# W in two transfers, gathered rows turned by every fourth column, and one store for row blocks 28 and 29

## The chip, the cores and the metric

The kernel runs on one core of a Trainium2 chip. The metric is the device time of one execution in microseconds (us). Before the change it is 235.61 us, the median of three runs (235.59 to 236.09).

## The reference

The reference is one layer of graph attention with four heads, a residual and a layer norm. `x` is 4096x512, `adj` 4096x4096, `W` 512x2048 (four heads of 512 columns) and `a` holds two vectors of 512 for each head, all fp32.

```python
ht = (h @ W).reshape(N, N_HEADS, N_HIDDEN).transpose(1, 0, 2)
src = jnp.einsum('hnd,hd->hn', ht, a_src)
dst = jnp.einsum('hnd,hd->hn', ht, a_dst)
e = jax.nn.leaky_relu(src[:, :, None] + dst[:, None, :], SLOPE) + adj_mat[None]
att = jax.nn.softmax(e, axis=-1)
h_prime = jnp.einsum('hij,hjd->hid', att, ht)
return h_prime.mean(axis=0)
...
x = _layernorm(x + _L0_gnn_ref(x, adj, L0_gnn_W, L0_gnn_a), axis=-1)
```

The entries of `adj` reach 1e9, so in nearly every row the softmax gives all its weight to the column with the largest entry. For such a row i with column j the result is `layernorm(x[i] + x[j] @ mean_of_heads(W))`.

## The kernel before, in words

`leading_rows` uses this. It finds the largest entry of each row of `adj`, gathers the row of `x` that it points to, multiplies it with the mean of W over the heads, adds `x` and normalises. At the end it tests whether the lead of the largest entry is large enough to make the softmax exact. Only if a row fails is `general` entered (L546 and following), which computes the attention in full; in these runs it is not.

**Row blocks.** The 4096 rows are 32 row blocks of 128. Row block `ib` holds in partition p the row 32p + ib. One loop over `t` from 0 to 31 is a pipeline written out by hand, without a scheduler: at step `t`

- SP (SyncE's queue) issues the load of `adj` block t + 5 (`load_adj`, L122: 2 MB, 16 KB in each partition) and, at some steps, a load of several row blocks of `x` (`load_x`, L125) into the long-lived tile `hold`. There are six buffers for `adj`; a load waits until VectorE is done with the block that was in its buffer.
- VectorE takes maxima of segments of 16 or 32 columns (`segment_maxima`, L169), finds the best segment (`find_segment`, L176 and L178), and from the segment fetched for block t - 2 the column (`find_column`, L208 and L214).
- GpSimd (POOL) fetches the best segment again (`fetch_segment`, L191) and gathers the rows of `x` into `y` (`gather_rows`, L202), both with an indirect DMA on its own queue. There are four buffers for `y`.
- TensorE turns block t - 3 (`turn`, L229: four transposes of 128x128), ScalarE copies the result to `yt` (L231), and TensorE adds the residual (`residual`, L237) and multiplies with `w_sum` (`products`, L244).
- ScalarE takes the sums for the layer norm and normalises (L266, L268, L251, L277), with GpSimd's help (L271 to L273).

**W.** W is loaded at the start into the upper half of `hold`, row blocks 16 to 31, which `x` overwrites later. It comes in four transfers of 1 MB (`load_w`, L128): transfer kb brings rows 128kb + p of W, one row of 8 KB in each partition p. `mean_of_heads(kb)` (L334, L335) adds its four heads on TensorE and writes `w_sum[:, kb]`. `turn_w` (L350) and `head_vector` (L358) form W times `a`, one (kb, head) at a time; `head_norms` (L364 and following) uses only their norms over all rows of W. `products` multiplies `yt[:, kb]`, the columns 128kb to 128kb + 127 of the gathered rows, turned, with `w_sum[:, kb]`, the rows of W of the same numbers.

**Order on SP at the start.** `adj` 0, W 0, `adj` 1, W 1, `adj` 2, W 2, `adj` 3, W 3, `adj` 4, `x` 0 to 3, then the loop's. ScalarE's queue carries two small loads of `a`. The transfers of both queues take eight completion semaphores in turn, so each waits until the one eight before it has landed.

**The tail.** After the loop the last blocks are written out by hand. Row block 31's column is found directly in the whole row (L222), its rows are gathered, turned and multiplied in two halves (`products_of_half`, L286), and normalised in halves by VectorE and ScalarE (L326). SP issues the stores (L329) in one fixed order: row blocks 0 to 7 in two stores of four, 8 to 23 in eight of two, then 28 alone, 29 alone, 24 and 25, 26 and 27, 30, and last 31. A row block of a store is 2 KB in each partition. The names at the tail are NB = 32, Q = 4, LATE = NB - Q = 28 and BEHIND = LATE - Q = 24.

Of the kernel before, what the change touches and what calls it, by code (L numbers as in the profile page):

```python
# [20 lines left out]
P = 128  # L21
# [7 lines left out]
def gat_resnorm_kernel(  # L29
# [29 lines left out]
    any_bad = keep.tile([1, 1], I32, name="any_bad")  # L59

    leading_rows(tc, x, adj, W, a, out, ident, v, n_bad, any_bad)

    flag = nc.values_load(any_bad[0:1, 0:1], min_val=0, max_val=N)
    with tc.If(flag > 0, preferred_fallthrough_block=True, label="general"):
        general(tc, x, adj, W, out, ident, v, n_bad)
# [3 lines left out]
def leading_rows(ctx, tc, x, adj, W, a, out, ident, v, n_bad, any_bad):  # L69
# [8 lines left out]
    nc = tc.nc  # L78
    N, D = x.shape
    H = a.shape[0]  # L80
    KB, NB, S = D // P, N // P, N // E
    S_EARLY = N // E_EARLY
    AHEAD = 5
    Q = 4
    PIECES = 4
    LATE = NB - Q
    BEHIND = LATE - Q
# [11 lines left out]
    adj_segs_early = adj.rearrange("n (s e) -> (n s) e", e=E_EARLY)  # L99
    x_rows = x.rearrange("(p nb) d -> p nb d", nb=NB)  # L100
    out_rows = out.rearrange("(p nb) d -> p nb d", nb=NB)
    w_blocks = W.rearrange("(kb p) (h d) -> p kb h d", p=P, h=H)


    once.tile([P, 24], F32, name="pad")
    hold = once.tile([P, NB, D], F32, name="hold")
    w_at = NB - KB * H
# [6 lines left out]
    def pieces(ib):  # L114
        return PIECES if ib == NB - 1 else 2 if ib >= LATE else 1

    def load_adj(ib):
        if 0 <= ib < NB:
            t = adj_t[ib] = adj_pool.tile([P, N], F32, name="adj_t")
            n = pieces(ib)  # L120
            for k in range(n):
                nc.sync.dma_start(t[:, ts(k, N // n)], adj_rows[ib][:, ts(k, N // n)])  # L122

    def load_x(lo, n):
        nc.sync.dma_start(hold[:, ds(lo, n), :], x_rows[:, ds(lo, n), :])  # L125

    def load_w(kb):
        nc.sync.dma_start(hold[:, ds(w_at + kb * H, H), :], w_blocks[:, kb])  # L128

    load_adj(0)  # L130
    for s in range(2):
        nc.scalar.dma_start(a_rows[ts(s, H), :], a[:, ts(s, D), :].rearrange("h d o -> h (d o)"))
    for kb in range(KB):
        load_w(kb)
        load_adj(kb + 1)
    load_x(0, Q)
    for ib in range(KB + 1, AHEAD):
        load_adj(ib)

    make_identity(nc, ident)  # L140
    first = once.tile([P, NB], U32, name="first")
# [83 lines left out]
    def turn(ib):  # L225
        y = y_t.pop(ib)
        tp = psum.tile([P, KB, P], F32, name="tp", bufs=2)
        for kb in range(KB):
            nc.tensor.transpose(tp[:, kb, :], y[:, ts(kb, P)], ident)  # L229
        yt = yt_of[ib] = rows.tile([P, KB, P], F32, name="yt")  # L230
        nc.scalar.copy(yt, tp)  # L231

# [89 lines left out]
    def finish_in_halves(ib):  # L322

        halves, i = o_ps.pop(ib), slice(ib, ib + 1)
        normalise(ib, halves[0], slice(0, D // 2))
        nc.scalar.activation(hold[:, ib, D // 2 :], halves[1], AF.Identity, bias=nm[:, i], scale=sd[:, i])  # L326

    def store(queue, lo, n):
        queue.dma_start(out_rows[:, ds(lo, n), :], hold[:, ds(lo, n), :])  # L329
# [93 lines left out]
    for t in range(NB):  # L423
# [29 lines left out]
        ib = t - PROJECT  # L453
# [6 lines left out]
        if ib >= 0:  # L460
            turn(ib)
            if ib > BEHIND:
                products(ib - 1, KB - 1, KB)
            if ib < BEHIND:
                residual(ib)
# [25 lines left out]
    add_x(nc.gpsimd, BEHIND + 2)  # L491
    products(LATE, KB - 1, KB)
    turn(NB - 3)
    residual_in_halves(NB - 1)
    products(NB - 3, 0, 1)
# [11 lines left out]
    bound(3)  # L507
    test()
    turn(NB - 2)
    stats(BEHIND + 2)  # L510
    rstd(slice(BEHIND, BEHIND + 3))
# [25 lines left out]
    moments(NB - 1)  # L537
    factor(NB - 1, shift=True)
    finish_in_halves(NB - 1)
    for ib, n in ((NB - 4, 1), (NB - 3, 1), (BEHIND, 2), (BEHIND + 2, 2), (NB - 2, 1)):  # L540
        store(nc.sync, ib, n)
    store(nc.sync, NB - 1, 1)

# [2 lines left out]
def general(ctx, tc, x, adj, W, out, ident, v, n_bad):  # L546
# [7 lines left out]
    nc = tc.nc  # L554
    N, D = x.shape
    KB, NB, NCH, Q = D // P, N // P, N // C, C // P
    H = v.shape[2] // 2

    const = ctx.enter_context(tc.tile_pool(name="const", bufs=1))
    x_sb = const.tile([P, NB, D], F32, name="x_sb")  # L560
# [4 lines left out]
    w_blocks = W.rearrange("(kb p) m -> p kb m", p=P)  # L565

    with ExitStack() as pre:
        sd_all = pre.enter_context(tc.tile_pool(name="all", bufs=1)).tile([2 * H, N], F32, name="sd_all")
        two = pre.enter_context(tc.tile_pool(name="two", bufs=2))
        pps = pre.enter_context(tc.tile_pool(name="pps", bufs=2, space=bass.MemoryType.PSUM))  # L570
        for g in range(NCH):
            nc.gpsimd.dma_start(x_sb[:, ts(g, Q), :], x_blocks[:, ts(g, Q), :])
        for kb in range(KB):
            nc.gpsimd.dma_start(w_sb[:, kb, :], w_blocks[:, kb, :])
        for g in range(NCH):
            xT = two.tile([P, KB, C], F32, name="xT")
            for q in range(Q):
                ps = pps.tile([P, KB, P], F32, name="ps_x")
                for kb in range(KB):
                    nc.tensor.transpose(ps[:, kb, :], x_sb[:, g * Q + q, ts(kb, P)], ident)  # L580
                nc.scalar.copy(xT[:, :, ts(q, P)], ps)
            ps = pps.tile([2 * H, C], F32, name="ps_sd")
            for kb in range(KB):
                nc.tensor.matmul(ps, v[:, kb, :], xT[:, kb, :], start=(kb == 0), stop=(kb == KB - 1))
            sd = sd_all[:, ts(g, C)]
            nc.vector.tensor_copy(sd, ps)
            for h in range(H):
                pb = pps.tile([P, C], F32, name="ps_b")
                one_hot = ident[: 2 * H, H + h : H + h + 1].to_broadcast([2 * H, P])
                nc.tensor.matmul(pb, one_hot, sd, start=True, stop=True)  # L590
                nc.vector.tensor_copy(dst_b[:, h, ts(g, C)], pb)
        for g in range(NCH):
            pt = pps.tile([P, Q, 2 * H], F32, name="ps_s")
            for q in range(Q):
                rows_of = sd_all[:, ds(g * Q + q, P, NB)]
                nc.tensor.transpose(pt[:, q, :], rows_of, ident[: 2 * H, : 2 * H])
            nc.vector.tensor_copy(src[:, ts(g, Q), :], pt[:, :, :H])
# [98 lines left out]
```

## Time and profile before

| | before |
|---|---|
| median of the runs | 235.61 us (235.59 to 236.09) |
| the profiled execution, whole | 235.65 us |
| its span, first to last instruction | 234.1 us |
| TensorE (PE) busy | 197.5 us, 84% |
| VectorE (DVE) busy | 191.6 us, 82% |
| ScalarE (ACT) busy | 111.6 us, 48% |
| GpSimd (POOL) busy | 100.3 us, 43% |
| DMA, mean rate over the span | 415 GB/s |
| median time from issue to landing, W | 18.8 us |
| median time from issue to landing, `adj`, 2 MB | 31.7 us |
| median time from issue to landing, gather of `y` | 7.7 us |

How to read the profile: it is one execution, and times in it count from its span's start. A page gives the busy time of each engine, then the span in 40 equal slices in which a digit is the busy share in tenths, then the DMA queues (packets, megabytes, share of the time of the 16 transfer engines). A group of instructions has its line, engine, operation, output and inputs, sizes and count; behind the first bar the busy time in us and the mean in ns; behind the second the engine's idle time just before, with what ended it. PEld is TensorE's loading of the stationary operand, which overlaps its matmuls. A row of the timeline has its start, its length, engine, line, operation and tiles, and in brackets the idle time before it and what ended that. The chain of waits is followed back from the last instruction, each step to what released it; its rows have start, length and what was waited for or worked on.

### The profile page before, as it was taken

The numbers are of one execution on the slowest core, as the hardware profiler recorded it, in microseconds if no ns is written. First come the engines' busy times: TensorE is split into PE (matmuls) and PEld (weight loads), VectorE is DVE, ScalarE is ACT, GpSimd is POOL, SyncE is SP. The second block draws the span as 40 slices with busy tenths as digits, with TensorE's granted clock in tenths as the row PEclk, the third lists the DMA queues.
The fourth block names the chain that finished last, engine by engine and source line by source line (L and its number), as shares of the span: only waits on it lengthen the run. The fifth ranks groups of instructions, "written<-read, shape, count | busy, mean of one in ns | idle before, by whom it ended". The sixth has DMA issues, their size and how long they took to land.

```text
span 234.1 us, 2486 instructions
## 1 busy us (share of the span) xinstructions
PE 197.5 (84%) x683; PEld 101.6 (43%) x683; DVE 191.6 (82%) x300; ACT 111.6 (48%) x267; POOL 100.3 (43%) x212
## 2 busy tenths in 40 slices
PE   0198959999999699999999599859899967999980
PEld 0034525765656356555544144324333423344360
DVE  0566885589929999999789986999999999989871
ACT  2003012155665447475768264645564654187561
POOL 2022232415524464646443642646465464557400
PEclk9999778999999999999999979999999999999997
DMA  6999999999999999999999999999999999999994
GB/s 243 432 428 417 445 419 434 418 444 420 433 422 427 430 424 433 426 419 431 434 427 427 429 433 424 419 436 419 435 428 417 425 427 421 413 426 419 416 386 179
DMA packets 12977, 97.06 MB, mean 415 GB/s; under 512 B 2072, under 2 KB 2584, under 8 KB 7200
## 3 DMA queue, kind: packets, MB, share of 16 engines
q1 hardware_dynamic: 9360, 88.08, 89.0%
q0 software_dynamic: 3584, 8.77, 9.5%
q8 instruction: 6, 0.10, 0.2%
q14 instruction: 11, 0.09, 0.1%
q10 hardware_dynamic: 16, 0.02, 0.0%
HBM read 88.47 MB, written 8.39 MB: 414 GB/s over the span
## 4 chain that ended last, share of the span: by engine, by line
DMA 48%; POOL 19%; issue 17%; DVE 11%; PE 2%; ACT 0%; POOLq 0%; DVEq 0%; ACTq 0%; SPq 0%
DMA adj_t<-in_adj_dram 41%; DVE seg L169 8%; POOL y L202 6%; POOL lead L191 5%; DMA y<-in_x_dram,col 3%; DMA lead<-in_adj_dram,row 2%; POOL sd L272 2%; PE o L286 2%; DMA a_rows<-in_L_gnn_a_dram 1%; DVE col L222 1%; POOL row L185 1%; POOL start L198 1%; POOL col L216 1%; POOL lead_early L191 1%; DVE at L178 1%
## 5 line engine op out<-in xcount | busy, mean ns | idle before, releaser
L169 DVE TENSOR_REDUCE seg<-adj_t 128x128 f32<-128x2048 f32 (+2 forms) x66 | 145.4, 2207 | 29.0 <-DMA adj_t<-in_adj_dram 29.0
L244 PE MATMUL o<-w_sum,yt 128*128 128x512 f32 x248 | 116.0, 609 | 0.7 <-ACT yt L231 0.7
L244 PEld LDWEIGHTS o<-w_sum,yt 128*128 128x128 f32 x248 | 44.8, 193 | 53.9 <-issue 42.4
L231 ACT COPY yt<-tp 128x512 f32<-128x512 f32 x32 | 18.8, 587 | 45.8 <-PE tp L229 45.7
L202 POOL DMA_INDIRECT y<-in_x_dram,col x32 | 30.8, 961 | 16.5 <-POOL col L216 15.4
L334 PE MATMUL o<-hold,ident 128*128 128x512 f32 x32 | 20.9, 815 | 14.6 <-DMA hold<-in_L_gnn_W_dram 14.6
L229 PE MATMUL tp<-ident,y 128*128 128x128 f32 x128 | 19.7, 276 | 13.7 <-DMA y<-in_x_dram,col 13.7
L237 PE MATMUL o<-hold,ident 128*128 128x512 f32 x52 | 26.8, 600 | 0.0
L229 PEld LDWEIGHTS tp<-ident,y 128*128 128x128 f32 x128 | 14.4, 141 | 26.8 <-issue 25.5
L185 POOL TENSOR_TENSOR row<-at,first 128x1 uint32<-128x1 uint32 x32 | 6.0, 188 | 43.7 <-DVE at L178 43.3
L352 ACT COPY wt<-tp 128x512 f32<-128x512 f32 x16 | 9.2, 586 | 31.5 <-PE tp L350 31.5
L191 POOL DMA_INDIRECT lead_early<-in_adj_dram,row x18 | 18.1, 1008 | 8.9 <-POOL row L185 8.9
L216 POOL TENSOR_TENSOR col<-start,within 128x1 uint32<-128x1 uint32 x31 | 5.8, 188 | 36.0 <-DVE within L214 36.0
L251 ACT ACTIVATE sq<-hold 128x512 f32<-128x512 f32 x32 | 19.8, 619 | 0.0
L358 PEld LDWEIGHTS pv<-at_d,wt 128*128 128x128 f32 x128 | 16.3, 191 | 6.8 <-ACT wt L352 3.7
L334 PEld LDWEIGHTS o<-hold,ident 128*128 128x128 f32 x32 | 8.1, 265 | 25.1 <-issue 20.2
L335 ACT ACTIVATE w_sum<-o 128x512 f32<-128x512 f32 x4 | 2.4, 598 | 33.0 <-PE o L334 33.0
L277 ACT ACTIVATE hold<-o,nm,sd 128x512 f32<-128x512 f32 x24 | 17.2, 769 | 0.0
L191 POOL DMA_INDIRECT lead<-in_adj_dram,row x14 | 14.0, 1003 | 7.0 <-POOL row L185 7.0
L268 ACT ACTIVATE sq<-o,nm 128x512 f32<-128x512 f32 x24 | 16.5, 687 | 0.8
L358 PE MATMUL pv<-at_d,wt 128*128 128x2 f32 x128 | 15.3, 244 | 0.6 <-ACT wt L352 0.6
L266 ACT ACTIVATE sq<-o 128x512 f32<-128x512 f32 x24 | 14.6, 609 | 0.0
(91 smaller groups left out, 150.8 us busy)
## 6 DMA issues: line engine op xcount, KB each, us to landing
adj_t<-in_adj_dram SPq DMA_DIRECT2D x28, 2048.0 KB, 31.7
adj_t<-in_adj_dram SPq DMA_DIRECT2D x6, 1024.0 KB, 28.0
out_dram<-hold SPq DMA_DIRECT2D x10, 512.0 KB, 14.3
hold<-in_L_gnn_W_dram SPq DMA_DIRECT2D x4, 1024.0 KB, 18.8
hold<-in_x_dram SPq DMA_DIRECT2D x2, 2048.0 KB, 36.5
hold<-in_x_dram SPq DMA_DIRECT2D x3, 1024.0 KB, 27.8
adj_t<-in_adj_dram SPq DMA_DIRECT2D x4, 512.0 KB, 19.7
out_dram<-hold SPq DMA_DIRECT2D x2, 1024.0 KB, 13.8
```

What stands on the lines that cost most here:

```text
L169: nc.vector.tensor_reduce(seg_of[ib][:, ts(k, N // e // n)], adj_t[ib][:, ts(k, N // n)].rearrange("p (s e) -> p s e", e=e), axis=AX.X, op ...
L191: nc.gpsimd.indirect_dma_start(out=lead, out_offset=None, in_=adj_segs_early if early else adj_segs, in_offset=bass.IndirectOffsetOnAxis(a ...
L202: nc.gpsimd.indirect_dma_start(out=y, out_offset=None, in_=x, in_offset=bass.IndirectOffsetOnAxis(ap=col[:, :1], axis=0),)
L229: nc.tensor.transpose(tp[:, kb, :], y[:, ts(kb, P)], ident)
L231: nc.scalar.copy(yt, tp)
L237: nc.tensor.matmul(o_ps[ib], ident, hold[:, ib, :], start=start, stop=False)
L244: nc.tensor.matmul(o_ps[ib], yt_of[ib][:, kb, :], w_sum[:, kb, :], start=(start and kb == 0), stop=(kb == KB - 1),)
L251: nc.scalar.activation(sq, hold[:, ib, :], AF.Square, accum_out=xx[:, ib : ib + 1])
L268: nc.scalar.activation(sq, o, AF.Square, bias=nm[:, i], accum_out=sd[:, i])
L277: nc.scalar.activation(hold[:, ib, :], o_ps.pop(ib), AF.Identity, bias=nm[:, i], scale=sd[:, i])
L334: nc.tensor.matmul(o, ident, hold[:, w_at + kb * H + h, :], start=(h == 0), stop=(h == H - 1))
L358: nc.tensor.matmul(pv[:, kb, h : 2 * H : H], wt[:, k, :], at_d[:, k, h : 2 * H : H], start=(k == 0), stop=(k == KB - 1),)
```

## The change

W's row 4p + kb now lies in partition p as its block kb, so that each partition's four rows are 32 KB in one piece. Two transfers of 2 MB bring two blocks each, 16 KB in each partition; `adj` 1 stands between them, and `adj` 2, 3, 4 and the first load of `x` behind them. To match, `turn` takes for its transpose kb the columns kb, kb + 4, kb + 8 and so on of the gathered rows, instead of 128 neighbouring ones (and `general` does the same with `x`). The stores of row blocks 28 and 29 become one.

```diff
-    w_blocks = W.rearrange("(kb p) (h d) -> p kb h d", p=P, h=H)
+    w_blocks = W.rearrange("(p kb) (h d) -> p (kb h) d", p=P, h=H)
...
-    def load_w(kb):
-        nc.sync.dma_start(hold[:, ds(w_at + kb * H, H), :], w_blocks[:, kb])
+    def load_w(kb, n):
+        nc.sync.dma_start(hold[:, ds(w_at + kb * H, n * H), :], w_blocks[:, ds(kb * H, n * H), :])
...
-    for kb in range(KB):
-        load_w(kb)
-        load_adj(kb + 1)
+    for kb in range(0, KB, 2):
+        load_w(kb, 2)
+        load_adj(kb // 2 + 1)
+    for ib in range(KB // 2 + 1, AHEAD):
+        load_adj(ib)
     load_x(0, Q)
-    for ib in range(KB + 1, AHEAD):
-        load_adj(ib)
...
-            nc.tensor.transpose(tp[:, kb, :], y[:, ts(kb, P)], ident)
+            nc.tensor.transpose(tp[:, kb, :], y[:, ds(kb, P, KB)], ident)
...
-    for ib, n in ((NB - 4, 1), (NB - 3, 1), (BEHIND, 2), (BEHIND + 2, 2), (NB - 2, 1)):
+    for ib, n in ((LATE, 2), (BEHIND, 2), (BEHIND + 2, 2), (NB - 2, 1)):
         store(nc.sync, ib, n)
...
-                    nc.tensor.transpose(ps[:, kb, :], x_sb[:, g * Q + q, ts(kb, P)], ident)
+                    nc.tensor.transpose(ps[:, kb, :], x_sb[:, g * Q + q, ds(kb, P, KB)], ident)
```

## The prediction

> **What bounds the kernel now.** I read the page's slices first, then its groups, then the chain of waits, then the timeline around the edited lines.
>
> ```profile
> DMA  6999999999999999999999999999999999999994
> DMA packets 12977, 97.06 MB, mean 415 GB/s; under 512 B 2072, under 2 KB 2584, under 8 KB 7200
> q1 hardware_dynamic: 9360, 88.08, 89.0%
> q0 software_dynamic: 3584, 8.77, 9.5%
> ...
> L169 DVE TENSOR_REDUCE seg<-adj_t 128x128 f32<-128x2048 f32 (+2 forms) x66 | 145.4, 2207 | 29.0 <-DMA adj_t<-in_adj_dram 29.0
> L229 PE MATMUL tp<-ident,y 128*128 128x128 f32 x128 | 19.7, 276 | 13.7 <-DMA y<-in_x_dram,col 13.7
> L229 PEld LDWEIGHTS tp<-ident,y 128*128 128x128 f32 x128 | 14.4, 141 | 26.8 <-issue 25.5
> ```
>
> The transfer engines are full from the second slice to the last but one: 89.0% plus 9.5% of the span is packet time. SP's queue (q1) is served in order, so a block of `adj` lands when all bytes ahead of it have passed. VectorE waits for nothing else in L169 (29.0 us in 13 waits), and TensorE waits for gathered rows. So the kernel is bound by the byte stream, with VectorE (191.6 us busy) close behind, and after the stream by a serial tail. The chain's end shows that tail:
>
> ```profile
> 204.23 5.55 DMA lead<-in_adj_dram,row
> ...
> 215.40 7.09 DMA y<-in_x_dram,col
> 222.49 0.14 issue
> 222.62 0.63 PE tp L229 x4
> 223.25 0.86 PE o L244 x2
> 224.11 3.55 PE o L286 x16
> ```
>
> Nothing else hides the four transposes of row block 31 (0.63 us); the last store is issued at 229.70, when its data is ready.
>
> Where does the stream hand over to the tail?
>
> ```profile
> 182.02 2.29 DVE L169 TENSOR_REDUCE seg<-adj_t 128x64 f32<-128x2048 f32 x1 [0.31 <-DMA adj_t<-in_adj_dram]
> ```
>
> This is block 27: VectorE waited 0.31 us for it, and from here runs without a wait until block 30's segment is found at 203.4, which releases the fetch at 204.23. So an earlier landing of block 27 moves the end one for one, up to 0.31 us; more than that meets VectorE's own pace.
>
> **What the Trainium skill says.** (1) "DMA: Bandwidth & Descriptors", Why small descriptors are slow: each packet carries a small fixed overhead. The packet records agree: medians of 611 ns for 16 KB, 309 for 8 KB, 159 for 4 KB, 84 for 2 KB, that is 7 to 9 ns each beside the bytes. (2) "Advanced Engine Details and Errata", SBUF Cachelines: lines of 16 bytes, "Need at least two hits on a cacheline to absorb SRAM access latency". Every fourth fp32 column is one hit per line. Nothing in this trace reads weights so; the price is open. (3) "TensorE: Matmul & The Clock Gate", its table: LDWEIGHTS is pulled ahead of matmuls in flight. The trace agrees: four loads of 141 ns fit in 0.42 us in the turn of block 31, and start about 109 ns apart, as the matmuls do.
>
> **The change, part by part.**
>
> *W in two transfers.* Each partition now takes two runs of 16 KB instead of four of 8 KB. Per transfer engine: 32 packets of 309 ns = 9.89 us become 16 of 611 = 9.78; two closing packets of 9 ns go: -0.13 us. A second reading, from consumers' starts:
>
> ```profile
> 8.36 4.48 DVE L169 TENSOR_REDUCE seg<-adj_t 128x128 f32<-128x2048 f32 x2 [8.36 <-DMA adj_t<-in_adj_dram]
> 10.87 6.47 PE L334 MATMUL o<-hold,ident 128*128 128x512 f32 x8 [10.87 <-DMA hold<-in_L_gnn_W_dram]
> 15.66 4.48 DVE L169 TENSOR_REDUCE seg<-adj_t 128x128 f32<-128x2048 f32 x2 [1.83 <-DMA adj_t<-in_adj_dram]
> 18.15 3.70 PE L334 MATMUL o<-hold,ident 128*128 128x512 f32 x8 [0.47 <-DMA hold<-in_L_gnn_W_dram]
> 23.02 2.29 DVE L169 TENSOR_REDUCE seg<-adj_t 128x128 f32<-128x2048 f32 x1 [1.88 <-DMA adj_t<-in_adj_dram]
> ```
>
> 1 MB of W takes 2.51 and 2.49 us, 2 MB of `adj` 4.79 and 4.87: at 16 KB packets two of W would take about 4.85 instead of 4.98, so at most -0.25 for all. I take -0.13, and 0 to -0.25 as its ends. It is on the path through block 27.
>
> *Order of the first transfers.* Ahead of `adj` block 1 there is 1 MB more (2.45 us), ahead of block 2 2 MB, ahead of block 3 1 MB, ahead of block 4 nothing. Blocks 1, 2, 3 land at 18.1, 27.9 and 32.8. VectorE needs 5.6 us for a block: 2 is done at 33.5, 3 at 39.1, 4 at 44.7, and block 5 lands at 47.6, where VectorE now waits 3.45 us. So this costs nothing; the cover is that wait. Without it the delay at block 4 would be 0.6 us (38.49 to 39.1). Later loads need a free buffer: block 9's is issued when VectorE is done with block 3, 38.1 instead of 35.1. Then blocks 5 to 8 and two loads of `x` are still in the queue, over 25 us of work, so it does not run dry. `load_x(0, Q)` stands behind block 4 as before. Each transfer on SP also waits for the one eight before it; with two fewer, this only lets SP issue earlier.
>
> *TensorE's start.* The first sums of heads begin at 13.2 instead of 10.87, the last at 22.9 instead of 33.63. Row block 0 is then turned when its rows have landed (gather issued at about 31.2, 7 us later, 38.5) instead of 42.44. By block 6 TensorE stands waiting for rows either way: this is worth nothing at the end. The heads' vectors come from the same instructions on other rows.
>
> *Turning by every fourth column.* `y` is the operand loaded as weights: in `turn_a` the load is 8x128, the width of `a_rows`, and the matmul 8x8. One load has 141 ns; a load of one column (L385) has 84, so 128 columns take about 57. The loads are hidden as long as they stay under the 109 ns spacing. Reading in steps touches the same elements, so a gain is excluded: lower end 0. At half rate 57 becomes 114: the first load shows 0.06 more and three spacings grow by 0.005: +0.07 us. At a quarter, as if each element cost a whole line, 57 becomes 228: 0.17 + 3 x 0.12 = +0.53. I take half, since the page's two-hit rule fits one hit at half speed, and keep 0 and 0.53. Only block 31's turn counts. Earlier turns have idle time ahead of them:
>
> ```profile
> 165.56 0.63 PE L229 MATMUL tp<-ident,y 128*128 128x128 f32 x4 [0.76 <-DMA y<-in_x_dram,col]
> ...
> 171.02 0.63 PE L229 MATMUL tp<-ident,y 128*128 128x128 f32 x4 [0.46 <-DMA y<-in_x_dram,col]
> ```
>
> +0.07 disappears in 0.46 to 0.76, and +0.53 just about fills it.
>
> *28 and 29 stored together.* Of three parts: SP issues one store fewer; per engine 16 packets of 84 ns become 8 of 159 (-0.07); and row block 28, issued at 217.32, goes out with 29 at 222.13. The stores behind wait for ScalarE and VectorE (issued at 225.31 and later), not for SP. Block 28's store landed 10.8 us after its issue, at 228.1; 29's, issued at 222.13, 6.7 us after, at 228.8: both stood behind older stores, so the pair should land near 228.8 too. The last store is set by its own data, at 229.70. Value 0; were the queue the bound there, -0.07.
>
> *General branch:* not run; nothing.
>
> Sum: -0.13 + 0.07 = -0.06. The profiled span of 234.1 becomes 234.04; 1.55 us lie around it (235.65 whole), and the median of the runs, 235.61, is 0.04 below that: 235.55. Both unknowns at their ends: -0.25 + 0 = 235.36; 0 + 0.53 = 236.14.
>
> **Rivals.**
> *Slower: the stepped weight load is dear.* For it: one hit per line, 128 loads, and block 31's turn is bare on the chain. Against: 50 ns of slack in each spacing. It decides from +0.60 on four transposes, i.e. from a spacing of about 0.25 us instead of 0.109. At sixfold cost of a column (57 to 342) the first shows 0.29, three others 0.23 each: +0.98, less 0.13: 236.5. TensorE would also exceed the 5.4 us a block that it has (4.9 busy + 0.98) and carry up to 1 us into the tail: at most 237.5.
>
> *Faster: the late gather is freed.* The fetch of `y` for block 31 takes 7.09 us while stores are queued. Taking 256 KB out of its way would give 0.25 MB at 415 GB/s = 0.63 us: 234.9. Against: 28's store landed at 228.1, after that gather's 222.49, so it was not ahead of it.
>
> *The packets do not join.* If the two transfers still go in 8 KB packets, the stream gains nothing: 235.7, no difference either. For joining speaks that `adj` rows of 16 KB go as one packet each.
>
> **How the numbers follow.** About 0.2% (0.47 us) is what a measurement of this kernel can tell from no change. My sum and both its ends: 0.65. Packets not joined: 0.07, also within. Dear weight load: 0.17, slower. Gather freed: 0.11, faster. So 0.11, 0.72, 0.17. The range takes in the freed gather at 234.9 and, above, the bounds of the sum and the nearer half of the dear load: 236.4.
>
> **What would show it.** SP's queue with about 430 packets fewer (256 of W, 128 of the store, 16 for each of three transfers); `adj` blocks 1 to 3 starting on VectorE near 18, 28 and 33.5, block 5 near 47.5 and block 27 near 181.9; the weight load of L229 near 200 ns, with four transposes under 0.75 us. I am wrong if that group takes 1.2 us or more, if TensorE stops waiting for `y` between 150 and 190, if block 5 starts after 48.5, or if the last gather's time moves by more than half a microsecond.

## The result, and the profile after

The changed kernel takes 235.23 us, the median of 22 runs (234.99 to 235.49), beside 235.61 us before (22 runs). The ratio is 0.9977, with a 95% interval of 0.9969 to 0.9985, so it is faster by about 0.2%: 0.38 us by the medians, 0.54 us by the ratio, which takes in the five runs from 236.06 to 236.95 us that only the kernel before had. The forecast was 235.55 in a range of 234.9 to 236.4, so the time lies in the range; but the forecast sum held only 0.06 us of gain.

The page of the changed kernel first. Behind a group's second bar stands the idle time ahead of it.

```profile
span 233.8 us, 2482 instructions
...
DMA packets 12545, 97.06 MB, mean 415 GB/s; under 512 B 2024, under 2 KB 2536, under 8 KB 7024
...
q1 hardware_dynamic: 8928, 88.08, 89.0%
...
L169 DVE TENSOR_REDUCE seg<-adj_t 128x128 f32<-128x2048 f32 (+2 forms) x66 | 145.4, 2207 | 28.1 <-DMA adj_t<-in_adj_dram 28.0
...
L229 PE MATMUL tp<-ident,y 128*128 128x128 f32 x128 | 21.9, 294 | 10.1 <-DMA y<-in_x_dram,col 9.9
...
L229 PEld LDWEIGHTS tp<-ident,y 128*128 128x128 f32 x128 | 18.8, 208 | 21.9 <-issue 20.6
```

SyncE's queue has 432 packets fewer (9360 - 8928), as forecast. The stepped weight load takes 208 ns in the mean instead of 141. The stream is as full as before.

VectorE's timeline at the start, and at block 27:

```profile
8.40 4.48 DVE L169 TENSOR_REDUCE seg<-adj_t 128x128 f32<-128x2048 f32 x2 [8.40 <-DMA adj_t<-in_adj_dram]
18.11 4.48 DVE L169 TENSOR_REDUCE seg<-adj_t 128x128 f32<-128x2048 f32 x2 [4.23 <-DMA adj_t<-in_adj_dram]
27.86 2.29 DVE L169 TENSOR_REDUCE seg<-adj_t 128x128 f32<-128x2048 f32 x1 [4.28 <-DMA adj_t<-in_adj_dram]
...
33.47 2.27 DVE L169 TENSOR_REDUCE seg<-adj_t 128x128 f32<-128x2048 f32 x1
...
39.06 2.27 DVE L169 TENSOR_REDUCE seg<-adj_t 128x128 f32<-128x2048 f32 x1
...
47.64 2.29 DVE L169 TENSOR_REDUCE seg<-adj_t 128x128 f32<-128x2048 f32 x1 [2.91 <-DMA adj_t<-in_adj_dram]
```

```profile
182.06 2.29 DVE L169 TENSOR_REDUCE seg<-adj_t 128x64 f32<-128x2048 f32 x1
```

Blocks 1 to 3 are late as worked out (18.1, 27.9, 33.5), and block 5 is at 47.64, where it was at 47.63. But block 27 starts at 182.06, not 0.13 us before 182.02. The tail of the chain of waits is then not shorter but longer:

```profile
204.27 5.57 DMA lead<-in_adj_dram,row
...
215.45 7.25 DMA y<-in_x_dram,col
222.69 0.14 issue
222.83 0.72 PE tp L229 x4
223.55 0.86 PE o L244 x2
224.41 3.55 PE o L286 x16
```

The four transposes take 0.72 us instead of 0.63, and the last store is issued at 230.00 instead of 229.70. Yet the span ends 0.3 us earlier. So the gain is made after the last store's issue. There SyncE waits for transfers and then executes its DRAIN instructions. For the kernel before, its waits from 229 on and its last instructions; then the same of the changed kernel:

```profile
SPq L691 <- DMA out_dram<-hold: 1.3, 2, 0.8
```

```profile
L691 SPq EVENT_SEMAPHORE  x14: 17/28/28, 231.2 to 234.0; - x14
L691 SPq DRAIN  x3: 7/7/7, 233.2 to 233.5; - x3
```

```profile
SPq L691 <- DMA out_dram<-hold: 0.6, 1, 0.6
```

```profile
L691 SPq EVENT_SEMAPHORE  x14: 17/28/28, 231.5 to 233.7; - x14
L691 SPq DRAIN  x3: 7/7/7, 232.9 to 233.2; - x3
```

The first drain moved from 233.2 to 232.9, with as many semaphore instructions. The single records of the trace show that SyncE checks the eight completion semaphores of the transfers (the counters by which a transfer reports that it has landed) one after the other, in a fixed order, 0.06 us each, and drains after the last. In these records the last store lands at 232.84 before and at 232.79 after, nearly the same. But before, its semaphore is the third of the eight: the five behind it, long done, are still checked, and the first drain comes at 233.23, 0.39 after the landing. In the changed kernel it is the eighth: the drain comes at 232.88, 0.08 after it.

Why the eighth? Transfers take the semaphores in turn. Before there are 67 (65 of SyncE, two of ScalarE), and 67 = 8 x 8 + 3. The change takes away two of W and one store: 64 = 8 x 8.

From this I formed three theories. *Exit*: the gain is the five checks. *Stream*: it comes from fewer and larger packets. *Chain*: what sets the end is block 31's data, as the prediction had it.

### The profile page after: what moved, and what is told of

Its sections match the earlier page's. It is cut to its first block, busy times and chain, and to the rows that moved or that the text cites. A ratio compares the mean times of both kernels' runs of the same rounds, so it can differ in the third digit from the quotient of the medians.

```text
span 233.8 us, 2482 instructions
## 1 busy us (share of the span) xinstructions
PE 201.5 (86%) x683; PEld 106.4 (46%) x683; DVE 191.5 (82%) x300; ACT 111.7 (48%) x267; POOL 100.3 (43%) x212
## 3 DMA queue, kind: packets, MB, share of 16 engines
q1 hardware_dynamic: 8928, 88.08, 89.0%
## 4 chain that ended last, share of the span: by engine, by line
PE 35%; DMA 23%; POOL 19%; issue 17%; DVE 2%; ACT 1%; POOLq 0%; DVEq 0%
PE o L244 20%; DMA hold<-in_x_dram 14%; POOL y L202 6%; POOL lead L191 5%; PE o L237 5%; PE pv L358 4%; DMA adj_t<-in_adj_dram 3%; DMA y<-in_x_dram,col 3%; PE tp L229 3%; DMA lead<-in_adj_dram,row 2%; POOL sd L272 2%; PE tp L350 2%; PE o L286 2%; DVE col L222 1%; POOL row L185 1%
## 5 line engine op out<-in xcount | busy, mean ns | idle before, releaser
L244 PE MATMUL o<-w_sum,yt 128*128 128x512 f32 x248 | 119.4, 624 | 0.7 <-ACT yt L231 0.7
L244 PEld LDWEIGHTS o<-w_sum,yt 128*128 128x128 f32 x248 | 46.4, 199 | 56.2 <-issue 44.8
L229 PE MATMUL tp<-ident,y 128*128 128x128 f32 x128 | 21.9, 294 | 10.1 <-DMA y<-in_x_dram,col 9.9
L237 PE MATMUL o<-hold,ident 128*128 128x512 f32 x52 | 28.8, 639 | 1.5 <-DMA hold<-in_x_dram 1.5
L334 PE MATMUL o<-hold,ident 128*128 128x512 f32 x32 | 17.6, 709 | 13.4 <-DMA hold<-in_L_gnn_W_dram 13.4
L229 PEld LDWEIGHTS tp<-ident,y 128*128 128x128 f32 x128 | 18.8, 208 | 21.9 <-issue 20.6
L358 PEld LDWEIGHTS pv<-at_d,wt 128*128 128x128 f32 x128 | 17.2, 200 | 7.4 <-issue 3.9
L334 PEld LDWEIGHTS o<-hold,ident 128*128 128x128 f32 x32 | 7.1, 229 | 21.5 <-issue 21.5
L358 PE MATMUL pv<-at_d,wt 128*128 128x2 f32 x128 | 16.0, 249 | 0.6 <-ACT wt L352 0.6
```

The source lines that it names most:

```text
L229: nc.tensor.transpose(tp[:, kb, :], y[:, ds(kb, P, KB)], ident)
L237: nc.tensor.matmul(o_ps[ib], ident, hold[:, ib, :], start=start, stop=False)
L244: nc.tensor.matmul(o_ps[ib], yt_of[ib][:, kb, :], w_sum[:, kb, :], start=(start and kb == 0), stop=(kb == KB - 1),)
L334: nc.tensor.matmul(o, ident, hold[:, w_at + kb * H + h, :], start=(h == 0), stop=(h == H - 1))
L358: nc.tensor.matmul(pv[:, kb, h : 2 * H : H], wt[:, k, :], at_d[:, k, h : 2 * H : H], start=(k == 0), stop=(k == KB - 1),)
```

## Experiments

In each run the kernel before ran beside it, with medians of 235.56 to 235.61.

**Position of the last store, from both sides.** Two kernels put the last store of the changed kernel back to the first semaphore, one by storing 28 and 29 apart, one by a load of 4 bytes.

```diff
-    for ib, n in ((LATE, 2), (BEHIND, 2), (BEHIND + 2, 2), (NB - 2, 1)):
+    for ib, n in ((NB - 4, 1), (NB - 3, 1), (BEHIND, 2), (BEHIND + 2, 2), (NB - 2, 1)):
```

> The changed kernel with row blocks 28 and 29 stored apart again, so 65 transfers instead of 64. Exit theory (what counts is how many completion semaphores SyncE still checks after the last store's): the last store goes from the eighth semaphore to the first, seven checks of 0.06 us follow it, so +0.42 us on the changed kernel: 235.65, as before the change. Stream theory (the gain comes from fewer and larger packets): only the pair's 0.07 us is lost, 235.3.

Measured: 235.73 us. Ratio to before 1.0004 (0.9998 to 1.0011). The whole gain is gone.

```diff
-    once.tile([P, 24], F32, name="pad")
+    pad = once.tile([P, 24], F32, name="pad")
...
         load_adj(t + AHEAD)
+        if t in (14,):
+            nc.sync.dma_start(pad[0:1, ds(t, 1)], W[0:1, ds(t, 1)])
```

> The changed kernel with one load of 4 bytes more at step 14, into an unused tile. The last store moves from the eighth semaphore to the first. Exit theory: +0.42 us, 235.65. Stream theory: 235.25.

Measured: 235.67 us, ratio 1.0003 (0.9996 to 1.0010). Four bytes at step 14, 120 us ahead of the end, take back the gain of a change of 4 MB. SyncE's longest wait at the end, and its drains:

```profile
SPq L693 <- DMA out_dram<-hold: 1.3, 1, 1.3
```

```profile
L693 SPq DRAIN  x3: 7/7/7, 233.3 to 233.6; - x3
```

It waits 1.3 us at the first semaphore, and still has seven to check. The next kernel gives the gain to the kernel before, whose W, turns and stores stay.

```diff
         load_adj(t + AHEAD)
+        if t in (6, 10, 14, 18, 22):
+            nc.sync.dma_start(pad[0:1, ds(t, 1)], W[0:1, ds(t, 1)])
```

> The kernel before with five loads of 4 bytes more on SyncE's queue, at steps 6, 10, 14, 18 and 22, into an unused tile; W, the turns and the stores as before. The last store moves from the third semaphore to the eighth. Exit theory: five checks of 0.06 us fall away, 235.61 - 0.30 = 235.3. Stream theory: no bytes are saved and five transfers added, 235.6 or a little more.

Measured: 235.34 us, ratio 0.9989 (0.9982 to 0.9996), 0.26 us less than the 235.60 beside it. The first drain comes at 232.9, as in the changed kernel:

```profile
L693 SPq DRAIN  x3: 7/7/7, 232.9 to 233.2; - x3
```

```diff
-    for ib, n in ((NB - 4, 1), (NB - 3, 1), (BEHIND, 2), (BEHIND + 2, 2), (NB - 2, 1)):
+    for ib, n in ((LATE, 2), (BEHIND, 2), (BEHIND + 2, 2), (NB - 2, 1)):
```

> The kernel before with row blocks 28 and 29 stored together, nothing else: 66 transfers instead of 67. Exit theory: the last store moves from the third semaphore to the second, one check more, +0.06: 235.67; with the 0.07 us of packet time saved 235.6. Stream theory: 235.54.

Measured: 235.66 us, ratio 1.0006 (0.9997 to 1.0016). Storing 28 and 29 together saves nothing that shows by itself.

Together, with the time from the last store's landing to the first drain from each trace's records:

| kernel | semaphore of the last store | landing to drain, us | median, us |
|---|---|---|---|
| e1, e3 | 1st | 0.51, 0.51 | 235.73, 235.67 |
| e5 | 2nd | 0.45 | 235.66 |
| before | 3rd | 0.39 | 235.61 |
| e2, changed | 8th | 0.08, 0.08 | 235.34, 235.23 |

The drain's distance falls by 0.06 us for each place. The medians follow it over the five and seven places; a single place, as in e5, is less than they can tell (e5's interval is 0.45 us wide). Exit stands; Stream falls as the main cause.

**The stepped turn.** One kernel takes it out of the change, one puts it into the kernel before.

```diff
-            nc.tensor.transpose(tp[:, kb, :], y[:, ds(kb, P, KB)], ident)
+            nc.tensor.transpose(tp[:, kb, :], y[:, ts(kb, P)], ident)
```

> The changed kernel with the gathered rows turned by neighbouring columns, so that the columns meet other rows of W than they should; all else is the same. Chain theory (block 31's turn is bare on the chain that sets the end): the four transposes take 0.63 us again instead of 0.72, so 0.09 us less, 235.14. If the last store waits for a transfer engine that is behind, and not for its data: 235.23.

Measured: 235.37 us, ratio to before 0.9992 (0.9983 to 1.0002): no gain on the changed kernel's 235.23.

```diff
-    w_blocks = W.rearrange("(kb p) (h d) -> p kb h d", p=P, h=H)
+    w_blocks = W.rearrange("(p kb) (h d) -> p kb h d", p=P, h=H)
...
-            nc.tensor.transpose(tp[:, kb, :], y[:, ts(kb, P)], ident)
+            nc.tensor.transpose(tp[:, kb, :], y[:, ds(kb, P, KB)], ident)
```

> The kernel before with W's row 4p + kb in partition p, still in four transfers of 8 KB runs in the old order, and the turn by every fourth column; stores as before. It isolates the stepped weight load; the last store keeps its third semaphore. Chain theory: +0.09 us, 235.70. If the last store waits for a transfer engine that is behind: 235.61.

Measured: 235.62 us, ratio 1.0008 (0.9992 to 1.0023). The load is dearer in this kernel and plain again in e4. First e6, then e4, with shortest, median and longest in ns:

```profile
L229 PEld LDWEIGHTS tp<-ident,y x128: 195/211/260, 42.6 to 222.7; 128*128 128x128 f32 x128
```

```profile
L229 PEld LDWEIGHTS tp<-ident,y x128: 137/141/225, 39.2 to 223.0; 128*128 128x128 f32 x128
```

So 70 ns more for a load, and 0.09 us more for block 31's turn, do not show at the end. These two runs alone could miss them: their intervals are 0.45 and 0.73 us wide, and e4's profiled execution took 235.14 us, the chain theory's number, though its median did not follow.

**Is the chain the bound at all?** Two kernels make block 31's data later, one makes it earlier.

```diff
     stats_of_half(NB - 1, 1)
+    stats_of_half(NB - 1, 0)
     moments(NB - 1)
```

> The changed kernel with VectorE taking the statistics of block 31's first half a second time, behind those of the second half: 0.43 us more between block 31's products and its normalisation. Chain theory: the end moves with it, 235.66. If a transfer engine that is behind sets the end, its margin covers part: the last store of the changed kernel was issued 0.30 us later than before and still landed 0.05 earlier, so 235.2 to 235.4.

Measured: 235.93 us, ratio to before 1.0007 (0.9992 to 1.0023): 0.7 us more than the changed kernel, above both expectations. In its profile the two statistics take 0.77 us in place of 0.44 for one, so the delay is 0.33 us and not 0.43. The last store is issued at 230.10 and lands at 233.20: 0.10 and 0.41 us later than in the changed kernel's profile.

> The kernel before with VectorE taking the statistics of block 31's first half a second time: 0.43 us more between its products and its normalisation. Chain theory: 235.61 + 0.43 = 236.04. If a transfer engine that is behind sets the end: in eight kernels the last store landed between 232.6 and 232.9 whether issued at 229.6 or 230.5, so the 0.43 from 229.70 are covered, 235.6 to 235.75.

The edit is the same, in the kernel before. Measured: 236.86 us, ratio 1.0050 (1.0028 to 1.0071), with runs from 236.06 to 238.15. This is not a clean price for the delay: in its profile VectorE had lost time in the middle, long before the edit.

```profile
127.29 0.19 DVE L370 TENSOR_REDUCE n<-px 128x8 f32<-128x32 f32 x1 [2.45 <-PE px L368]
...
128.04 2.27 DVE L169 TENSOR_REDUCE seg<-adj_t 128x128 f32<-128x2048 f32 x1
```

Block 17 starts at 128.04 here, at 123.27 in the first profile. Besides the 2.45 us for TensorE in the line above, VectorE waited 2.68 and 0.79 us for fetched segments at 108.55 and 115.09. TensorE's granted clock was 0.92 from 40 to 108 us (1.00 in the first profile); but it was 0.92 in the changed kernel's profile too, where block 17 starts at 123.98, so the clock alone does not explain the loss. Its cause stays open. The four lowest runs, 236.06 to 236.23, lie 0.5 to 0.7 above the median beside them. So in these two kernels the later statistics cost at least their delay.

```diff
-            st = halves_st
+            st = halves_st[:, 0, :]
...
-    stats_of_half(NB - 1, 1)
     moments(NB - 1)
```

> The changed kernel with block 31's mean and variance taken from its first half alone, the second half's statistics left out, so that they are ready before the products of the second half end. Block 31's data are then ready when ScalarE has normalised the second half behind the last product, 227.95 + 0.6 = 228.5 instead of 230.0 in the profile. Chain theory: the end comes 1.4 us earlier, 233.8. If a transfer engine that is behind sets the end: 235.1 to 235.25.

Measured: 235.35 us, ratio to before 0.9991 (0.9983 to 0.9999). The end of its chain, and SyncE's wait behind it:

```profile
228.32 0.17 DVE nm L308
228.49 0.02 issue
228.51 0.02 ACTq L326
228.53 0.05 issue
228.57 0.56 ACT hold L326
```

```profile
SPq L690 <- DMA out_dram<-hold: 1.2, 2, 0.6
```

Its last store is issued at 229.16 and lands at 232.75, 3.6 us later; in the changed kernel 230.00 and 232.79. So it is issued 0.84 us earlier and lands 0.04 us earlier: the store before it was still under way and landed at 232.07. Making the data earlier gains nothing, where the chain theory asked for 1.4 us. The chain is not what sets the end. Nor does a later issue lengthen it by itself: the two kernels with merged stores below issue their last stores at 230.5 and land them within 0.04 us of the changed kernel's 232.79. What cost 0.7 us in e7 is therefore not shown.

**What the last store waits for.** In the windows of the kernel before (the last two columns are the mean share of the 16 transfer engines and GB/s):

```profile
231.00:231.50 0.50, 0.00 (x0) 0.00 (x0) 0.00 (x0) 0.00 (x0) 0.00 (x0) 1.00 0.51 189
231.50:232.00 0.50, 0.00 (x0) 0.00 (x0) 0.00 (x0) 0.00 (x0) 0.00 (x0) 0.55 0.07 29
232.00:232.50 0.50, 0.00 (x0) 0.00 (x0) 0.00 (x0) 0.00 (x0) 0.00 (x0) 0.50 0.06 25
```

A share of 0.06 is one engine of sixteen. It sends the last store's eight packets of 2 KB one behind the other until 232.2, when the others have been done for some 0.8 us. In the changed kernel one engine is left again:

```profile
231.50:232.00 0.50, 0.00 (x0) 0.00 (x0) 0.00 (x0) 0.00 (x0) 0.00 (x0) 0.50 0.17 62
232.00:232.50 0.50, 0.00 (x0) 0.00 (x0) 0.00 (x0) 0.00 (x0) 0.00 (x0) 0.50 0.06 25
```

The trace also records sixteen completions for each of these stores. In the kernel before, the sixteenth comes 0.15 to 0.36 us behind the fifteenth for the stores that land between 212.9 and 219.8, and 0.98 to 1.34 us behind for every store that lands from 222.7 on. So one of the sixteen is behind long before the last store.

Two kernels merge stores ahead of it, so that the queue carries fewer and larger packets; each also has loads of 4 bytes as in e2 that keep the last store on the eighth semaphore.

```diff
-    for ib in range(0, 2 * Q, Q):
-        store(nc.sync, ib, Q)
-    for ib in range(2 * Q, BEHIND, 2):
-        store(nc.sync, ib, 2)
+    for ib in range(0, BEHIND, Q):
+        store(nc.sync, ib, Q)
```

> The changed kernel with row blocks 8 to 23 stored in four stores of four blocks instead of eight of two, and four loads of 4 bytes more at steps 10, 14, 18 and 22, so that the last store keeps the eighth semaphore. Per transfer engine 64 packets of 159 ns become 32 of 309: 0.29 us less in the queue ahead of the last stores. If a transfer engine that is behind sets the end: 234.95. Chain theory and exit theory: 235.23.

Measured: 235.51 us (234.89 to 237.14), ratio to before 1.0006 (0.9988 to 1.0024).

```diff
-    for ib in range(2 * Q, BEHIND, 2):
-        store(nc.sync, ib, 2)
+    for ib, n in ((8, 4), (12, 2), (14, 2), (16, 2), (18, 2), (20, 4)):
+        store(nc.sync, ib, n)
```

> The changed kernel with row blocks 8 to 11 and 20 to 23 each in one store of four, and two loads of 4 bytes at steps 10 and 14 so that the last store keeps the eighth semaphore. Per transfer engine 32 packets of 159 ns become 16 of 309: 0.14 us less. If a transfer engine that is behind sets the end: 235.09. Chain theory: 235.23, or later if the late gather waits longer behind larger packets, as with all the stores in fours.

Measured: 235.31 us, ratio to before 0.9992 (0.9980 to 1.0003). Neither gains on the changed kernel. In their profiles the last stores are issued at 230.53 and 230.47 and land at 232.83 and 232.75, only 2.3 us later: there the one engine's lag is nearly gone, but the data are half a microsecond later, so the landing stays. Why the data are later there was not followed up.

> The changed kernel with the prefetch hint for the branch to the general part on SyncE too, as the other four engines have it. In all the profiles so far but two, an instruction fetch of 8 KB is recorded 0.36 to 0.45 us behind SyncE's branch, while one transfer engine sends the last store's packets 0.5 to 0.9 us behind the other fifteen. If that fetch holds the engine up and the hint takes it away: the last store lands 2.3 us after its issue, as in the two kernels without such a lag, instead of 2.8 to 3.1: 234.75. If the lag has another cause, or the fetch stays: 235.23.

```diff
-HINTED = tuple(getattr(mybir.EngineType, name) for name in ("PE", "Activation", "DVE", "Pool"))
+HINTED = tuple(getattr(mybir.EngineType, name) for name in ("PE", "Activation", "DVE", "Pool", "SP"))
```

Measured: 235.31 us, ratio to before 0.9989 (0.9980 to 0.9997). The fetch stays, 0.4 us behind SyncE's branch, and the landing stays too (issued at 230.09, landed at 232.74), though here four of the sixteen trail, and not one. The records show that this fetch does not begin the lag: in the kernel before, the branch comes at 230.96 and the fetch at 231.37, while one of the sixteen is behind from 222.7 on; and the two kernels with merged stores have the fetch at the same distance from the branch without the lag. What begins the lag stays open.

No variant beats the changed kernel.

## Why the prediction was right, point by point

**The direction and the size.** It called the likeliest outcome a gain of 0.06 us, within 0.2%. The medians differ by 0.38 us, 0.16%; the ratio says 0.23%, with 0.2% inside its interval. The range held it, but the sum lacked its largest term: its two terms, -0.13 and +0.07, did not make the gain. That the forecast held is in part luck.

**The step that failed** is in "Order of the first transfers": "Each transfer on SP also waits for the one eight before it; with two fewer, this only lets SP issue earlier." With the merged store it is three fewer, and the count also decides which of the eight semaphores the last store gets, and by that how many checks stand between its landing and the end. From third to eighth that is 5 x 0.06 = 0.30 us, of a total of 0.38; e2 shows 0.26 of it without any other part of the change, and e1 and e3 lose 0.50 and 0.44 for seven checks (0.42). To what the other 0.08 belongs stays open; it is less than these runs can tell.

**W in two transfers, -0.13.** The packets went as worked out, but at the end I find between nothing and 0.1 us, and this for all of the change but the semaphore's place. With the same semaphore, the changed kernel is 0.11 under e2; e1 and e3, at the first, are 0.00 and 0.06 under the kernel before carried to the first (235.61 + 2 x 0.06 = 235.73). Block 27 does not show it: it starts between 181.8 and 182.2 in four profiles with four transfers of W (before, e2, e5, e6) and between 181.7 and 182.7 in nine with two (181.7 to 182.3 in changed, e1, e3, e4, e7 and e8, 182.5 to 182.7 in e9, e11 and e12). The disturbed e10 is left out. A term of 0.13 is below what one profile can show there. "An earlier landing of block 27 moves the end one for one" was not shown, and with the end set as it is, it need not hold.

**The stepped turn, +0.07.** The size held: half the rate was assumed, 198 ns by that working, and 208 were measured; the turn grew by 0.09. The Trainium skill's "Advanced Engine Details and Errata", section on SBUF cachelines, states a penalty where each access meets another line, without a size; the trace agrees that there is one. But its place was wrong: "Only block 31's turn counts" took the chain for the bound. e9 shows that data 0.84 us earlier gain nothing at the end, and e4 and e6, within their wide intervals, show no cost.

**"The last store is set by its own data"** is the second wrong step. It was read from the issue, which follows the data at once. The landing was not looked at: 3.1 us later in the kernel before, 2.3 in e8 and e11, which lack the lag.

**28 and 29 stored together, 0.** As bytes it is nothing (e5); as a count it is one place, in the changed kernel the place from the first semaphore to the eighth. It is the edit that decides: e1 undoes it alone, and the gain is gone.

**The first transfers, 0.** Right; block 5 covers them. TensorE's first sums began at 13.4 and block 0 was turned at 38.7, as forecast; the last sums began at 25.4, not 22.9. What this is worth at the end was not tested.

**The rivals.** The dear weight load and the freed gather did not come. The last gather took 7.25 us instead of 7.09, and between 150 and 190 us TensorE still waits for gathered rows, 3.8 us in three waits (5.7 in six before).

## What to carry to other kernels

Count what is left after the last store has been issued, not only what leads to it: the landing on the slowest transfer engine, then the exit. If the exit checks completion semaphores in a fixed order, the number of transfers modulo their number is worth up to 0.4 us here, whatever the transfers carry; before explaining a gain of a few tenths, move that number with a tiny transfer. And test a chain from both sides: if earlier data gain nothing, the chain's end is not the bound, however bare it looks.

## What the runs showed that I had not expected

- SyncE's checks at the exit cost 0.06 us each even for transfers long done: 0.51 us from landing to drain with the last store on the first of eight semaphores, 0.08 on the eighth.
- In eight of the fourteen profiles the sixteenth completion of the last store comes alone, 0.4 to 1.0 us behind the fifteenth; in e7 and e10 two trail, in e9 and e12 several by less, in e8 and e11 hardly any. In all but e7 and e10 a last store issued anywhere from 229.2 to 230.5 lands between 232.6 and 232.9. Instruction fetches of 8 KB are recorded next to the late packets (at 231.4 and 232.2 before, at 231.7 and 232.2 after). Whether they share an engine is not shown.
- Delaying block 31's data by 0.33 us cost 0.7 us (e7). In its profile a fetch comes at 231.85, amid the last store's packets, not behind them, two engines trail, and the store lands 0.4 later. That the fetch is the reason is argued from one profile.
- A weight load by every fourth fp32 column takes 208 ns in the mean against 141, and four transposes start 120 ns apart in place of 109.
